# A four-level perceiver kernel: level 0's keys in a new written order, layernorm rows evicted by VectorE, level 3's values dealt out anew

## The chip, the core and the metric

The kernel runs on one core of a Trainium2 chip. The metric is device time in microseconds (us) of one execution; less is better. The core's engines are called by the profile's names: PE (TensorE matmul) with PEld (its weight loads), DVE (VectorE), ACT (ScalarE), POOL (GpSimd) and SP (SyncE, which issues most DMAs). PE writes its results to PSUM, from where DVE or ACT evict them into SBUF.

## What is computed

128 rows x of width 256 (2 batches of 64 latents) pass through twelve residual steps, in four levels of three. Each step adds a function of the layernormed rows:

```
for level in 0..3:
    x = x + xattn(layernorm(x), ctx)   # cross-attention over 2 x 1024 context rows of width 192
    x = x + attn(layernorm(x))         # a mixing of the latents, another kind in each level
    x = x + ffn(layernorm(x))          # a mixture of 8 experts, top 2
```

Three of them matter here. **Level 0's cross-attention** layernorms the context rows too, projects keys from them, divides every 64-wide head of a key by its root mean square, and appends the latents' own keys and values to the context's:

```
k = rmsnorm(heads(layernorm(ctx) @ Wk)) * kn_g
attn = softmax(where(mask, q @ k.T, -max));  out = attn @ v
```

**Level 1's mixing** is a weighted sum over the next 32 rows of the same batch, `out[l] = sum_d softmax(x @ W + b)[l, d] * x[l + d]`. **Level 3's cross-attention** needs `ctx @ Wv`, which depends on no latent and can be computed at any earlier time.

## The kernel before

Everything is fp32. One 128-row tile holds all latents, so each step is a chain of small operations on PE, DVE and ACT, and work that hangs on no latent is put into the gaps of that chain.

**Order.** A Tile scheduler places the instructions on the engines. Inside `in_written_order()` the instructions of PE, DVE, ACT and POOL are tied, engine by engine, to the order in which the program writes them; all of level 0's cross-attention stands inside it, and so does level 1's mixing, while level 1's expert step does not. Each engine works through its queue in order, so an instruction that waits holds up all behind it. DMA issues on SP are not tied.

**Fillers.** A generator such as `kv1.values(b, t)` or `kv3.keys(b, c)` makes a piece of another level's keys or values; `steps(work, n)` advances it by n steps. `values` (line 411) has three: 8 matmuls (`context_values`, lines 373 and 375), 8 more, then one eviction of 128x1024 by ACT (line 437). It takes a PSUM tile of two banks from `two_banks()`, of which there are two (three inside the attention of levels 1 and 3), and gives it back when its eviction is done.

**Level 0's keys** are made in four groups g of four 128-row pieces, and a fifth group, LAT, for the latents. The steps are small functions:

- `project(g)`: 16 matmuls into two banks (lines 373, 375);
- `statistics(g)`: four `bn_stats` and `bn_aggr` on DVE (lines 879, 880), a square root on ACT (line 219), a reciprocal on DVE (line 222), giving `rstd`;
- `take(g)`: four scaled evictions of the projection on DVE (line 901), which need `rstd`; they write one of two `kq` tiles;
- `squares(g)` on ACT (line 911), `sums(g)`: a reduction on DVE (line 916) and a square root on ACT (line 919);
- `over_rms(g)`: three DVE operations (lines 923, 924, 926); `turn_keys(g)`: 8 transposes on PE (line 935) and two evictions on ACT (line 949);
- `normalise_rows(g)` on POOL (line 959), needed only by the later weighing.

`scores(k)`, `softmax(k)`, `turn_p(k)`, `weigh(k)` follow for four units a to d; units a and b need groups 0 and 1 only. ACT's function table is switched by `table_for` (line 214), which runs a one-element activation, `junk`, right behind a table load.

**Turned rows.** `transposed(layernorm(x), 2)` transposes the layernormed rows by two PE transposes (line 247) and evicts them with `evacuate`, which takes DVE (line 102) and ACT (line 104) in turn by a toggle. `layernorm(x, then=F)` puts a square root and then the table load for F on ACT.

**Level 1's attention**, `narrow_attention`, runs 8 rounds over 16 units; each round has on ACT two exponentials (line 1308) and three evictions of transposed weights (line 1332), and PSUM is split so that only two single banks serve transposes (line 1323) and weighing (line 1349). Of level 3's values, the pieces (0,0), (0,2) and (1,0), two halves each, are the fillers from there to level 1's expert step: a half in round 6, one after the last weighing, one ahead of the mixing's layernorm, two after its router matmul, one after its band matmul (line 1495).

**Level 3's experts** run five rounds r; `ways_back()` makes, once, the transposed weights that `scatter(r)` uses, and ends in a matmul (line 755) that waits for an ACT copy (line 754).

Of the kernel before, what the change touches and what calls it, by code (L numbers as in the profile page):

```python
# [11 lines left out]
AF = mybir.ActivationFunctionType  # L12
# [5 lines left out]
P = 128  # L18
# [39 lines left out]
def tile_perceiver(ctx: ExitStack, tc: tile.TileContext, i: dict, out: bass.AP):  # L58
# [39 lines left out]
    def evacuate(dst, src):  # L98

        turn[0] ^= 1  # L100
        if turn[0]:
            nc.vector.tensor_copy(dst, src)  # L102
        else:
            nc.scalar.copy(dst, src)  # L104
# [135 lines left out]
    def transposed(src, n, pool=tok, tag="xT", name="xT"):  # L240

        t = pool.tile([P, n, P], F32, tag=tag, name=name)
        for at in range(0, n, 4):
            m = min(4, n - at)
            ps = bank()
            for c in range(m):
                nc.tensor.transpose(  # L247
                    ps[:, c * P : (c + 1) * P], src[:, (at + c) * P : (at + c + 1) * P], ident
                )
            evacuate(t[:, at : at + m, :].rearrange("p c t -> p (c t)"), ps[:, : m * P])  # L250
        return t
# [127 lines left out]
    class NarrowKeys:  # L379
# [33 lines left out]
        def values(self, b, t):  # L413

            ps = two_banks()
            for u in range(2):
                context_values(ps, self.wv, b, t, (u,))
                yield
            self.evict_values(
                self.v[:, b, :, t : t + 2, :], ps.rearrange("p (n t d) -> p n t d", n=2, t=2)  # L420
            )
            yield
# [131 lines left out]
    def experts(name, x, consts, shelf, blocks, pool, acc, less_sums, bias, b2, sums):  # L554
# [202 lines left out]
        for r in range(OVER + 1):  # L757
            if r:
                sums = sums_of(consts, own_over if r == OVER else consts.of_pair[r])
            prod = hidden(r, sums)  # L760
            if r == 0:
                shelf.load(2)
                shelf.load(3)
            turn(r, prod, 0)
            if r:
                out_of(r - 1)
            if r < OVER:
                gather(r + 1)
            turn(r, prod, 1)
            if r == 0:  # L770
                plan_blocks()
            if r == 1:
                ways_back()
            if r:
                scatter(r - 1)
# [11 lines left out]
    with psum(2, 4), stage_pool(name="l0x", bufs=1) as pool, stage_pool(  # L787
# [288 lines left out]
        statistics(0)  # L1076
        key_bias()
# [7 lines left out]
        statistics(1)  # L1085
        over_rms(LAT)
        sums(0)
        turn_keys(LAT)
        normalise_rows(0)
        normalise_rows(1)  # L1090
        mask_rows()
        a, b, c, d = ((b, j) for b in range(NB) for j in range(2))
        for g in range(4):

            if g > 0 and g < 3:
                statistics(g + 1)
                sums(g)
# [3 lines left out]
            else:  # L1101
                sums(3)
                table_for(AF.Exp, rn[3][:, 0:1])
                scores(a)
                normalise_rows(2)
                normalise_rows(3)
# [3 lines left out]
            if g < 3:  # L1110
                steps(kv1.values(g // 2, 2 * (g % 2)))
            turn_keys(g)
        softmax(a)
# [119 lines left out]
    with psum(2, 4), stage_pool(name="l0f", bufs=2) as pool:  # L1233
        with in_written_order():
            xl = layernorm(x, then=AF.Gelu)
            steps(fill[3], 1)
            xlT = transposed(xl, 2)
# [19 lines left out]
    def narrow_attention(pool, att, x, wq, bq, bv, kv, gap, tail=()):  # L1257
# [120 lines left out]
        with in_written_order():  # L1378
            steps(gap, 3)
            xlT = transposed(layernorm(x, then=AF.Exp), 2)  # L1380
# [8 lines left out]
            for r in range(rounds):  # L1389
# [28 lines left out]
                if r == rounds - 2:  # L1418
                    steps(tail, 1)
# [16 lines left out]
    fill = [kv3.values(0, 0), kv3.values(0, 2), kv3.values(1, 0)]  # L1436
# [14 lines left out]
    with psum(2, 4), stage_pool(name="l1a", bufs=1) as pool, in_written_order():  # L1451
        steps(fill[1], 1)
        xl = layernorm(x, then=AF.Exp)
        xlT = transposed(xl, 2)
# [17 lines left out]
        steps(fill[1])  # L1472
# [51 lines left out]
    with psum(2, 4), stage_pool(name="l2x", bufs=1) as pool, stage_pool(  # L1524
# [5 lines left out]
        with in_written_order():  # L1530
# [3 lines left out]
            xlT = transposed(layernorm(x, then=AF.Exp), 2)  # L1534
# [110 lines left out]
    with psum(2, 4), stage_pool(name="l2t", bufs=1) as pool, stage_pool(  # L1645
# [63 lines left out]
        with in_written_order():  # L1709
            fill = [kv3.keys(0, 0), kv3.keys(0, 1)]  # L1710
            steps(fill[0], 3)
            xlT = transposed(layernorm(x), 2)
# [302 lines left out]
    with psum(2, 4), stage_pool(name="l2f", bufs=2) as pool:  # L2015
        with in_written_order():
            last = kv3.keys(1, 0)
            steps(last, 3)
            xlT = transposed(layernorm(x, then=AF.Silu), 2)
# [53 lines left out]
    with psum(2, 3), stage_pool(name="l3a", bufs=1) as pool:  # L2073
        with in_written_order():
# [4 lines left out]
            xlT = transposed(layernorm(x, then=AF.Sigmoid), 2)  # L2079
# [212 lines left out]
```

## Time and profile before

| | |
|---|---|
| three timed runs | 735.01, 738.56, 739.65 us, median 738.56 |
| the profiled execution, its own time | 738.08 us |
| its span, first to last instruction | 736.4 us |
| mean granted TensorE clock | 0.966 |
| PE, DVE, ACT, POOL busy | 92%, 39%, 36%, 9% of the span |
| level 0's cross-attention | 0 to 90 us of the span, its key preparation to about 53 |
| level 1's attention, mixing, start of its experts | 149 to 201, 201 to 214, 214 to 228 us |
| level 3's experts | 648 us to the end |

A row of a timeline gives the start and the busy time in us, engine, line, operation, output <- inputs, shapes and count; the bracket at its end is the idle time of that engine before it and what ended it. A row of the windows view gives a stretch of the span, then the busy us of PE, PEld, DVE, ACT and POOL with their instruction counts, the granted clock of TensorE (1.00 or 0.50), and the DMA share and rate. The row PEclk of the page shows the same clock in tenths over 40 slices of 18.4 us.

### The profile page before, as it was taken

Reading aid. Unit: us, or ns where it says so; the run is one execution under the profiler, and the core shown is the slowest. Engines: PE = TensorE matmul, PEld = TensorE weight load, DVE = VectorE, ACT = ScalarE, POOL = GpSimd, SP = SyncE. Lnnn points to the kernel's source line nnn. Section 1 sums busy time; section 2 is a strip of 40 time slices with the busy share of each in tenths; the row PEclk is TensorE's granted clock in tenths of the full one; section 3 lists DMA queues with packets and bytes.
Section 4 is the critical chain, followed back from the end, with each engine's and each line's share of the span. In section 5 each row is a group of like instructions: output and inputs, shape, how many; then the busy total and the mean of one; then the engine's idle time right before and its main releaser. Section 6 shows DMA issues by size and latency. Waiting matters only on the chain.

```text
span 736.4 us, 11294 instructions
## 1 busy us (share of the span) xinstructions
PE 676.3 (92%) x4628; PEld 497.2 (68%) x4628; DVE 284.6 (39%) x719; ACT 268.4 (36%) x544; POOL 66.6 (9%) x92
## 2 busy tenths in 40 slices
PE   7779979989969999999999988999999989779997
PEld 3446657946639997576676587999989856544443
DVE  5853443157541003334333335534322267533111
ACT  2353252258543243233232424405231278431111
POOL 3530100000100000000000030030000000000250
PEclk9999999989988999999999999999999999959999
DMA  9930012840004887100000400011138800447881
GB/s 282 423 152 1 8 44 86 291 166 1 3 1 168 293 281 291 53 1 1 1 1 0 172 1 1 1 58 58 58 117 305 308 16 2 161 197 299 341 326 69
DMA packets 19302, 92.76 MB, mean 126 GB/s; under 512 B 3042, under 2 KB 5620, under 8 KB 10324
## 3 DMA queue, kind: packets, MB, share of 16 engines
q1 hardware_dynamic: 16976, 85.70, 31.5%
q0 software_dynamic: 2016, 6.30, 2.3%
q8 instruction: 36, 0.59, 0.3%
q14 instruction: 14, 0.11, 0.0%
q10 hardware_dynamic: 260, 0.06, 0.0%
HBM read 98.20 MB, written 0.13 MB: 134 GB/s over the span
## 4 chain that ended last, share of the span: by engine, by line
PE 83%; DVE 7%; ACT 6%; issue 2%; DMA 0%; POOL 0%; DVEq 0%; ACTq 0%; POOLq 0%
PE bank L255 34%; PE two_banks L574 5%; PE two_banks L1580 4%; PE bank L1323 4%; PE bank L247 3%; PE two_banks L1294 3%; PE bank L619 2%; PE two_banks L1585 2%; PE bank L1349 2%; PE two_banks L1752 2%; PE two_banks L373 2%; PE bank L1872 2%; PE two_banks L399 1%; PE two_banks L255 1%; ACT pT L1332 1%
## 5 line engine op out<-in xcount | busy, mean ns | idle before, releaser
L255 PEld LDWEIGHTS bank<-l2x_ctx,pT 128*128 128x128 f32 x256 | 42.2, 190 | 7.9 <-ACT pT L104 4.9
L255 PE MATMUL bank<-l2x_ctx,pT 128*128 128x192 f32 x256 | 44.4, 327 | 0.6 <-ACT pT L104 0.6
L348 DVE SCALAR_TENSOR_TENSOR x_new<-bank,comb,x_new 128x256 f32<-128x256 f32 x24 | 11.6, 484 | 80.0 <-PE bank L255 80.0
L1323 PEld LDWEIGHTS bank<-ident,p 128*128 128x128 f32 x256 | 29.6, 149 | 18.4 <-issue 6.8
L1323 PE MATMUL bank<-ident,p 128*128 128x128 f32 x256 | 39.5, 298 | 1.2 <-ACT pT L1332 0.5
L1302 DVE TENSOR_REDUCE negmax<-two_banks 128x1 f32<-128x1024 f32 x32 | 37.6, 1216 | 7.3 <-PE two_banks L1294 7.3
L1308 ACT ACTIVATE p<-two_banks,negmax 128x1024 f32<-128x1024 f32 x32 | 36.1, 1127 | 0.8 <-DVE negmax L1302 0.8
L1580 PE MATMUL two_banks<-ctxA,l2x_qA 128*128 128x512 f32 x64 | 32.6, 597 | 0.5 <-DVE l2x_qA L102 0.5
L255 PEld LDWEIGHTS bank<-xT,l1f_w_sb 128*128 128x128 f32 x256 | 32.5, 207 | 0.6 <-issue 0.3
L255 PE MATMUL bank<-xT,l1f_w_sb 128*128 128x128 f32 x256 | 32.8, 291 | 0.0
L1332 ACT COPY pT<-bank 128x512 f32<-128x512 f32 x48 | 26.9, 588 | 15.7 <-PE bank L1323 15.7
L1511 ACT ACTIVATE l1f_hT<-bank,cols 128x128 f32<-128x128 f32 x64 | 18.3, 368 | 35.6 <-PE bank L255 35.6
L255 PEld LDWEIGHTS bank<-xT,l2f_w_sb 128*128 128x128 f32 x256 | 29.6, 192 | 0.3
L255 PE MATMUL bank<-xT,l2f_w_sb 128*128 128x128 f32 x256 | 29.8, 275 | 0.0
L104 ACT COPY pT<-bank 128x512 f32<-128x512 f32 (+1 forms) x22 | 12.1, 557 | 47.8 <-PE bank L247 47.8
L255 PE MATMUL bank<-l1f_w_sb,l1f_hT 128*128 128x256 f32 x128 | 28.8, 379 | 0.0
L1590 DVE TENSOR_REDUCE negmax<-two_banks 128x1 f32<-128x1024 f32 x16 | 19.6, 1225 | 20.8 <-PE two_banks L1585 20.8
L1294 PE MATMUL two_banks<-n_kT,n_qx 32*128 32x512 f32 x128 | 25.0, 680 | 2.8 <-ACT n_kT L434 1.8
L247 PEld LDWEIGHTS bank<-ident,p 128*128 128x128 f32 x164 | 17.7, 141 | 13.8 <-issue 11.8
L255 PEld LDWEIGHTS bank<-l1f_w_sb,l1f_hT 128*128 128x128 f32 x128 | 23.8, 190 | 2.9
L574 PE MATMUL two_banks<-l3f_w_sb,m_xg 128*64 128x512 f32 (+1 forms) x112 | 25.0, 668 | 0.5 <-ACT m_xg L597 0.5
L262 POOL TENSOR_TENSOR x_bias<-x_new,rows 128x256 f32<-128x256 f32 x4 | 2.9, 726 | 242.1 <-DVE x_new L348 237.6
(559 smaller groups left out, 1316.5 us busy)
## 6 DMA issues: line engine op xcount, KB each, us to landing
l1f_w_sb<-in_l1f_w_dram SPq DMA_DIRECT2D x16, 1024.0 KB, 4.8
l3f_w_sb<-in_l3f_w_dram SPq DMA_DIRECT2D x12, 1024.0 KB, 5.7
more_w<-in_l3f_w_dram SPq DMA_DIRECT2D x12, 1024.0 KB, 11.2
l0f_w_sb<-in_l0f_w_dram SPq DMA_DIRECT2D x8, 1024.0 KB, 9.0
l2f_w_sb<-in_l2f_w_dram SPq DMA_DIRECT2D x8, 1024.0 KB, 4.7
l2f_w_sb<-in_l2f_w_dram SPq DMA_DIRECT2D x8, 512.0 KB, 4.6
xh<-in_ctx_dram SPq DMA_DIRECT2D x8, 192.0 KB, 6.0
l2x_ctx<-in_ctx_dram SPq DMA_DIRECT2D x1, 1536.0 KB
```

The costliest lines, as they stand in the source:

```text
L247: nc.tensor.transpose(ps[:, c * P : (c + 1) * P], src[:, (at + c) * P : (at + c + 1) * P], ident)
L255: nc.tensor.matmul(dst, lhsT, rhs, start=(k == 0), stop=(k == len(pairs) - 1))
L373: nc.tensor.matmul(dst[n], ctxA[:, b, n, keys], w[:, 0, :], start=True, stop=False)
L574: nc.tensor.matmul(part[s], xg[r][:, c, s], shelf.at[r, j, n](c, f), start=False, stop=(c == 1), skip_group_check=True,)
L1294: nc.tensor.matmul(sc[u][:, n * 512 : (n + 1) * 512], qx[rows_, c, n, b].rearrange("p h q -> p (h q)"), kT[c, b][rows_, n, :], start=True, ...
L1302: nc.vector.tensor_reduce(sc[u][1], sc[u][0], AX.X, ALU.max, negate=True)
L1308: nc.scalar.activation(p[u], sc[u][0], AF.Exp, bias=sc[u][1], scale=1.0, accum_out=total[u // 4][:, u % 4 : u % 4 + 1],)
L1323: nc.tensor.transpose(ps[:, kc * P : (kc + 1) * P], p[u][:, (4 * k + kc) * P : (4 * k + kc + 1) * P], ident,)
L1332: nc.scalar.copy(dst, ps)
L1511: nc.scalar.activation(hT[:, at + f, :], ps[:, f * P : (f + 1) * P], AF.Gelu, bias=col("l1f_b1", e * 8 + at + f), scale=1.0,)
L1580: nc.tensor.matmul(dst[n], qA[:, j, b].rearrange("p h q -> p (h q)"), ctxA[:, b, n, :], start=True, stop=False,)
L1590: nc.vector.tensor_reduce(negmax, sc, AX.X, ALU.max, negate=True)
```

## The change

Four edits. (1) `evacuate` gets `on_vector`; a new helper `turned_rows` evicts the two transposed layernorm blocks by DVE at nine places (levels 0 and 1's experts, level 1's mixing, both narrow attentions, level 2's three steps, level 3's mixing). The toggle still turns, so no other eviction changes its engine. (2) Level 0's key preparation is written in another order: statistics of group 1 go ahead of the first `take`, later statistics behind the sums of the group before; each value filler is split in two around `turn_keys`, its second half and its eviction now behind; scores and softmax of unit a go ahead of group 3's `over_rms`. (3) Level 3's first piece of values becomes two half pieces with an eviction each, by the new `values_of`; none is left in round 6 of level 1's attention, and three halves stand where the mixing's DVE chain runs, for two before. Level 1's expert step gets a written order for its layernorm. (4) `ways_back` of level 3's experts moves ahead of `out_of(0)` in round 1.

```diff
-    def evacuate(dst, src):
+    def evacuate(dst, src, on_vector=False):
         turn[0] ^= 1
-        if turn[0]:
+        if turn[0] or on_vector:
             nc.vector.tensor_copy(dst, src)
...
+    def turned_rows(xl):
+        return transposed(xl, 2, on_vector=True)
...
+        def values_of(self, b, t):
+            ps = two_banks()
+            context_values(ps, self.wv, b, t, (0,))
+            yield
+            self.evict_values(
+                self.v[:, b, :, t, :], ps.rearrange("p (n t d) -> p n t d", n=2, t=2)[:, :, 0]
+            )
+            yield
...
             turn(r, prod, 0)
+            if r == 1:
+                ways_back()
             if r:
                 out_of(r - 1)
...
-            if r == 1:
-                ways_back()
             if r:
                 scatter(r - 1)
...
         statistics(0)
+        statistics(1)
         key_bias()
...
         squares(0)
         sums(LAT)
-        statistics(1)
         over_rms(LAT)
         sums(0)
-        turn_keys(LAT)
         normalise_rows(0)
         normalise_rows(1)
         mask_rows()
+        turn_keys(LAT)
         a, b, c, d = ((b, j) for b in range(NB) for j in range(2))
         for g in range(4):
-            if g > 0 and g < 3:
-                statistics(g + 1)
-                sums(g)
             if g < 3:
                 take(g + 1, psk)
                 squares(g + 1)
             else:
-                sums(3)
-                table_for(AF.Exp, rn[3][:, 0:1])
-                scores(a)
-                normalise_rows(2)
-                normalise_rows(3)
+                softmax(a)
             if g < 2:
                 psk = project(g + 2)
             over_rms(g)
             if g < 3:
-                steps(kv1.values(g // 2, 2 * (g % 2)))
+                fill = kv1.values(g // 2, 2 * (g % 2))
+                steps(fill, 1)
+                sums(g + 1)
+            if g < 2:
+                statistics(g + 2)
+                normalise_rows(g + 2)
+            if g == 2:
+                table_for(AF.Exp, rn[3][:, 0:1])
             turn_keys(g)
-        softmax(a)
+            if g == 2:
+                scores(a)
+            if g < 3:
+                steps(fill)
         scores(b)
...
-            xlT = transposed(layernorm(x, then=AF.Exp), 2)
+            xlT = turned_rows(layernorm(x, then=AF.Exp))
...
-                if r == rounds - 2:
-                    steps(tail, 1)
...
-    fill = [kv3.values(0, 0), kv3.values(0, 2), kv3.values(1, 0)]
+    fill = [kv3.values_of(0, 0), kv3.values_of(0, 1), kv3.values(0, 2), kv3.values(1, 0)]
...
         steps(fill[1], 1)
         xl = layernorm(x, then=AF.Exp)
-        xlT = transposed(xl, 2)
+        xlT = turned_rows(xl)
         ps = bank()
         accumulate(ps[:, :32], [(xlT[:, c, :], router("l1a", c)) for c in range(2)])
-        steps(fill[1], 1)
-        steps(fill[2], 1)
+        steps(fill[1])
+        steps(fill[2], 2)
...
         nc.scalar.activation(w, w, AF.Exp, bias=nm, scale=1.0, accum_out=tot)
-        steps(fill[1])
+        steps(fill[2])
+        steps(fill[3], 1)
...
         nc.tensor.matmul(ps[:, :D], bandT[:, 0, :], xl, start=True, stop=True)
-        steps(fill[2], 1)
+        steps(fill[3], 1)
         x = residual(x, ps[:, :D])
-        steps(fill[2])
...
-        xlT = transposed(layernorm(x, then=AF.Gelu), 2)
+        with in_written_order():
+            xl = layernorm(x, then=AF.Gelu)
+            steps(fill[3])
+            xlT = turned_rows(xl)
         mix = Mix(x, gate(xlT, "l1f"))
```

More of the change, by code (lines that the diff above doesn't have):

```diff
@@ L238, in layernorm, with transposed @@
         return t
-    def transposed(src, n, pool=tok, tag="xT", name="xT"):
+    def turned_rows(xl):
+        return transposed(xl, 2, on_vector=True)
+    def transposed(src, n, pool=tok, tag="xT", name="xT", on_vector=False):
         t = pool.tile([P, n, P], F32, tag=tag, name=name)
@@ L249, in transposed @@
                 )
-            evacuate(t[:, at : at + m, :].rearrange("p c t -> p (c t)"), ps[:, : m * P])
+            evacuate(
+                t[:, at : at + m, :].rearrange("p c t -> p (c t)"), ps[:, : m * P], on_vector
+            )
         return t
@@ L420, in values @@
                 self.v[:, b, :, t : t + 2, :], ps.rearrange("p (n t d) -> p n t d", n=2, t=2)
+            )
+            yield
[5 more added lines that the diff above has]
+                self.v[:, b, :, t, :], ps.rearrange("p (n t d) -> p n t d", n=2, t=2)[:, :, 0]
             )
@@ L1453, in tile_perceiver @@
         xl = layernorm(x, then=AF.Exp)
-        xlT = transposed(xl, 2)
+        xlT = turned_rows(xl)
         ps = bank()
         accumulate(ps[:, :32], [(xlT[:, c, :], router("l1a", c)) for c in range(2)])
-        steps(fill[1], 1)
-        steps(fill[2], 1)
+        steps(fill[1])
+        steps(fill[2], 2)
         PAD = 32
@@ L1495, in tile_perceiver @@
         nc.tensor.matmul(ps[:, :D], bandT[:, 0, :], xl, start=True, stop=True)
-        steps(fill[2], 1)
+        steps(fill[3], 1)
         x = residual(x, ps[:, :D])
-        steps(fill[2])
     with psum(2, 4), stage_pool(name="l1f", bufs=2) as pool:
-        xlT = transposed(layernorm(x, then=AF.Gelu), 2)
+        with in_written_order():
+            xl = layernorm(x, then=AF.Gelu)
+            steps(fill[3])
+            xlT = turned_rows(xl)
         mix = Mix(x, gate(xlT, "l1f"))
@@ L1533, in tile_perceiver @@
             steps(last, 2)
-            xlT = transposed(layernorm(x, then=AF.Exp), 2)
+            xlT = turned_rows(layernorm(x, then=AF.Exp))
             steps(last)
@@ L1711, in tile_perceiver @@
             steps(fill[0], 3)
-            xlT = transposed(layernorm(x), 2)
+            xlT = turned_rows(layernorm(x))
             psk = project(1)
@@ L2018, in tile_perceiver @@
             steps(last, 3)
-            xlT = transposed(layernorm(x, then=AF.Silu), 2)
+            xlT = turned_rows(layernorm(x, then=AF.Silu))
             steps(last)
@@ L2078, in tile_perceiver @@
             nc.scalar.mul(less_sums, ps[:, :8], -1.0)
-            xlT = transposed(layernorm(x, then=AF.Sigmoid), 2)
+            xlT = turned_rows(layernorm(x, then=AF.Sigmoid))
             psz = features(xlT, wz, 0, 2)
```

## The prediction

> **What bounds the kernel.** The page first: who is busy, and what the chain that ended last is made of.
>
> ```profile
> PE 676.3 (92%) x4628; PEld 497.2 (68%) x4628; DVE 284.6 (39%) x719; ACT 268.4 (36%) x544; POOL 66.6 (9%) x92
> ...
> PEclk9999999989988999999999999999999999959999
> ...
> PE 83%; DVE 7%; ACT 6%; issue 2%; DMA 0%; POOL 0%; DVEq 0%; ACTq 0%; POOLq 0%
> ```
>
> PE carries 83% of the chain, DVE and ACT 13%, DMA nothing. The change removes no matmul, so it can gain in two ways: PE waits less for DVE and ACT, or PE runs less at half clock (the 8s and the 5 of PEclk). Both are read by stage. First the timeline of level 0's preparation, where I look at the brackets.
>
> ```profile
> 31.36 1.27 ACT L949 ACTIVATE kT<-bank,cols 128x512 f32<-128x512 f32 x2
> 32.52 0.30 ACT L219 ACTIVATE root<-cx_mv,eps 128x4 f32<-128x4 f32 x1
> ...
> 32.92 0.18 DVE L222 RECIPROCAL rstd<-root 128x4 f32<-128x4 f32 x1 [2.19 <-ACT root L219]
> ...
> 49.96 0.17 DVE L923 TENSOR_SCALAR rn<-rn 128x16 f32<-128x16 f32 x1 [2.54 <-ACT junk L214]
> ...
> 51.83 1.82 PE L935 MATMUL bank<-ident,kq 128*128 128x128 f32 x8 [1.17 <-DVE kq L926]
> ```
>
> A group's square root stands on ACT behind the key evictions of the group before, so DVE waits 2.19 us for it (2.50 in the next group), and in the last group 2.54 us behind the table load. Then the timeline of level 1, from the attention's end to the experts:
>
> ```profile
> 191.32 1.03 PE L373 MATMUL two_banks<-l3x_wv_sb,ctxA 128*128 128x256 f32 x4
> ...
> 194.24 1.08 PE L1349 MATMUL bank<-pT,n_v 128*32 128x128 f32 x32 [0.24 <-ACT pT L1332]
> ...
> 212.25 0.32 PE L247 MATMUL bank<-ident,l1a_band 128*128 128x128 f32 x1 [2.61 <-DVE l1a_band L1489]
> ...
> 217.58 1.28 ACT L214 ACT_TABLE_LOAD   x1
> ...
> 219.39 1.02 PE L255 MATMUL bank<-routers,xT 128*128 128x8 f32 x4 [2.52 <-ACT xT L104]
> ```
>
> The turned rows of level 1's experts wait on ACT behind a value copy and a table load. Last the windows view, cut into 3.41 us stretches on the grid of the clock's changes:
>
> ```profile
> 48.54:51.95 3.41, 2.24 (x11) 1.20 (x10) 1.92 (x4) 1.38 (x2) 0.00 (x0) 1.00 0.00 0
> 51.95:55.37 3.42, 3.42 (x11) 2.38 (x11) 1.22 (x3) 2.37 (x5) 0.00 (x0) 0.50 0.00 0
> ...
> 215.79:219.21 3.42, 1.09 (x7) 0.50 (x6) 0.46 (x2) 2.63 (x4) 0.00 (x0) 1.00 0.00 0
> 219.21:222.62 3.41, 3.23 (x15) 3.23 (x16) 1.57 (x11) 0.34 (x2) 0.00 (x0) 0.50 0.00 0
> 222.62:226.03 3.41, 3.41 (x18) 3.41 (x18) 0.00 (x0) 1.14 (x4) 0.00 (x0) 0.50 0.00 0
> ...
> 683.42:686.83 3.41, 2.75 (x14) 1.10 (x16) 0.13 (x1) 0.60 (x2) 0.00 (x0) 1.00 0.98 408
> 686.83:690.25 3.42, 3.42 (x10) 0.97 (x8) 0.00 (x0) 0.53 (x1) 0.00 (x0) 0.50 1.02 431
> ```
>
> After a stretch in which PE idles, or runs matmuls of 1 or 8 rows (lines 549's and 993's kind), the next comes at half clock, and it falls on dense work.
>
> **Part by part.** I sum against the profiled execution: 738.08 us, span 736.4.
>
> *Level 0's order.* I step the queues by the rows' durations: statistics 1.84 us, take 1.58 to the next (1.66 to its end), sums 1.2, over_rms 1.75, half a value piece 1.65, a projection 3.3, turn_keys 1.1, two key evictions 1.27, a value eviction 1.0. Stepped so, the old order gives 52.5 for the last turn_keys (trace: 51.83), so I trust differences. Statistics of group 1 (13.4 to 15.3) fit the 2.73 us in which DVE waited for the key bias until 16.16: nothing, if the rows are there; their last DMA issue ends at 7.89 and lands at most 6.0 later, 13.9. Then DVE is through LAT's over_rms 1.8 us earlier (20.3 for 22.1), and the first take starts near 23.6 for 25.24. From there DVE hardly waits: the root has only a short one ahead of it. But PE pays: the first value piece is evicted behind the key evictions, these behind the root (30.6 on ACT), so projection 3, which needs a two-bank tile, starts at 32.5 for 31.52, with PE idle from 30.0. The backlog (3.3 + 3.3 + 1.1 + 1.65 + 1.1, and 1.0 for the next value eviction) puts unit a's scores at 43.9 for 47.28, its softmax on DVE at 47.4, group 3's over_rms behind it at 49.4, the last turn_keys at 50.7 less the model's 0.65: **50.1 for 51.83, -1.7 us**. Which tile the planner hands out isn't in the trace: if projection 3 takes the other one and the third piece need not wait, -2.9; if all the slack goes to PE's waits, 0. I take -1.7. The POOL operations moved (normalise_rows) have until 60 us; SP gets no other order.
>
> *Level 1's attention.* Half a piece leaves round 6: 1.6 us of PE (191.32 to 192.91). What is late next is ACT: exponential 15 ends at 192.47, the eviction that frees the bank for line 1349 would run 192.5 to 193.05 instead of from 193.60. **-1.1.** The rounds behind keep their shape.
>
> *The mixing.* The half piece's own eviction is 0.6 us (128x512, as line 1332's rows) for 1.01, so the square root's table is there in time: -0.15 (root 203.61 while its input was ready at 203.43). Three halves, for two, now stand behind the router's matmul and the exponential, 5.0 us of PE from 204.9 to 209.8 in the shifted timeline; the band is ready at 210.8, so DVE's twelve band steps hide them with 1.0 us to spare, and each microsecond over that would count in full.
>
> *The turned rows.* From PE's transposes to the next matmul: 0.96 us through DVE (150.12 to 151.08), 0.90 through an idle ACT (413.99 to 414.89). Four of nine places were on DVE already. Level 2's and 3's two ACT places lose 0.06 each; level 0's gains 0.07; the mixing's 1.13 becomes 0.96, -0.17; level 1's experts' 2.95 (216.44 to 219.39) becomes 0.96, **-2.0**, and 0.1 more as the transposes no longer wait for the half piece on PE. The value copy that is written there now lies behind the table load on ACT, and its first gelu comes microseconds later. A rule speaks against this: the Trainium skill, *VectorE: DVE Perf Modes*, Specifications, places ScalarE closer to PSUM and VectorE closer to SBUF. By the rule the edit costs, at five places 0.06, +0.3 in all; the row of 2.95 outweighs it, because ACT's copy stands in a queue. The price of that queue differs too: *ScalarE: Activation LUTs*, What ACT_TABLE_LOAD costs, gives about 2.66 us for a switch, 1.38 of it a drain; here the load takes 1.28 and the next activation starts at 218.88, 0.02 later, so the gain is 2.0 and not the 3.4 that the page would make of it.
>
> *ways_back.* Its wait for the ACT copy (0.71 us ahead of 684.08) moves to about 678.8, behind two 0.59 us ACT copies: 0.7 again. Order alone: 0, bounds -0.7 (copy hidden) and +0.6 (one more ACT copy waited for).
>
> Sum of order and eviction: -1.7 - 1.1 - 0.15 - 0.17 - 2.1 + 0.05 = **-5.2**.
>
> *The clock.* Four of its half-clock spells fall where the change works. In level 0, turn_keys takes 1.82 for 1.09 and the scores' main part 2.85 for 1.88: 1.7. At the band matmul, 1.22 for 0.6: 0.6. At the experts' start, 6.6 us of dense PE at half clock: 3.3. In level 3, 32 matmuls of line 574 take 8.78 for 7.09: 1.7. Together **7.3**. The new order fills the stretches before them: unit a's scores and a half piece run where PE idled (43.8 to 46.3); the mixing's 3.3 us hole (208.93 to 212.25) is cut to 1.0, the 2.95 us one to under 1; ways_back no longer adds its 1.06 us of small work to the 8-row matmuls. Here a rule and the rows differ: the Trainium skill, *TensorE: Matmul & The Clock Gate*, What's actually happening, has the half clock after an idle window of about 3.4 us. By the rule only the level 1 spells could go (the stretches ahead of the others hold 2.24 and 2.75 us of busy PE): 3.9. By the rows weak stretches count as well: 7.3. Against that, the new idle 2.4 us ahead of projection 3 could draw a spell, 1.7. The page also says that the windows run free of the kernel, which no run here shows yet; but the grid is arbitrary to the program, so I count two thirds: **-4.8**.
>
> 738.1 - 5.2 - 4.8 = 728.1; the profiled execution lies 0.5 under the median, so **728.5**.
>
> **The rivals.**
>
> *The clock gives nothing* (0.20): spells are lost here and come elsewhere. For it: nine spells in the trace, five of them in places that the change leaves. Against: the two in level 1 follow PE holes of 3.3 and 2.95 us, and both are closed. 738.6 - 5.2 = 733.4, a no-change by measurement.
>
> *Level 0 gives nothing* (0.06): PE's waits for tiles eat the 1.7, and a spell takes the place of the old one. 728.5 + 1.7 + 1.1 = 731.3.
>
> *Slower by a clinging half clock* (0.04): a spell can hold itself, since slow work leaves weak stretches; 645.87 to 662.94 is five in a row. If PE's idle time ahead of projection 3 starts such a spell in level 0, its 16.6 us of PE work to the last turn_keys doubles, less PE's idle time of 2.4, 1.2 and 1.6 us: +11.4 there, and the level 0 gains (1.7 and 1.7, the second by two thirds) are gone: 728.5 + 11.4 + 2.8 = 742.7. It decides from some five windows on; in the trace PE's hole there of 2.3 us (19.9 to 22.26) started none.
>
> That the change doesn't do what it says, by other tiles or by order left to the planner, lies in level 0's bounds.
>
> **How the numbers follow.** Forecast 0.70 (726 to 731), the rivals 0.20, 0.06, 0.04. Low: everything comes, with the other tiles: 738.1 - 5.2 - 1.2 - 7.3 = 724.4, less 0.9 for another run's grid: 723.5. High: order without clock, 733.4, and 1.6 for the three runs' own spread: 735. About 1% (7.4 us) is what a measurement of this kernel can tell from no change. Faster by more: under 731.2, the forecast and a third of the second rival, 0.72. Within: 0.24. Slower: 0.04.
>
> **What would show it.** In the changed profile: the last turn_keys of level 0 near 50; DVE without 2 us waits for roots; PE idle some 2 us ahead of projection 3, with its releaser a value eviction on ACT or a take; in round 7 line 1349 at 1.1 us sooner; turned rows by line 102's copy nine times, router matmul within 1.0 us of the transposes; no 0.50 in the stretches behind the mixing; round 2's 32 matmuls near 7.1 us. I am wrong if level 1's experts start less than 3 us nearer to the attention's end, if new spells at half clock appear in level 0, or if the band's transpose waits for value matmuls.

## The result and the profile after

The changed kernel took **728.3 us** (median of four executions, 727.30 to 731.73) for 738.5 before (735.01 to 739.65): a ratio of 0.9869, 95% interval 0.9831 to 0.9907. Its profiled execution took 727.3 us, with a span of 725.6, 10.8 under that of before, and a mean granted clock of 0.976 for 0.966. First the page of the changed kernel: busy time, the clock in 40 slices, and the chain that ended last.

```profile
PE 670.8 (92%) x4628; PEld 493.7 (68%) x4628; DVE 286.9 (40%) x724; ACT 266.6 (37%) x540; POOL 65.9 (9%) x92
...
PEclk9899999989999999999999999999999999969999
...
PE 85%; DVE 8%; ACT 5%; issue 2%; DMA 0%; POOL 0%; DVEq 0%; ACTq 0%; POOLq 0%
```

The same 4628 matmuls are busy for 5.5 us less, and the span has 34.6 us at half clock for 49.5 before, so about half of the 10.8 us is clock. The 8 in the second slice is new. To see where the time came from, I matched the matmuls of the two traces and followed the distance between their starts:

| from here on | before, us | after, us | shift | new |
|---|---|---|---|---|
| level 0, weights of unit a turned | 58.67 | 57.92 | -0.75 | -0.75 |
| level 0, experts | 121.27 | 118.97 | -2.30 | -1.55 |
| level 1, projection of the attention | 201.16 | 197.46 | -3.70 | -1.40 |
| level 1, band's transpose | 212.25 | 208.84 | -3.41 | +0.29 |
| level 1, experts' router | 219.39 | 213.44 | -5.95 | -2.54 |
| level 1, experts, some 6 us on | 228.38 | 219.26 | -9.12 | -3.17 |
| level 3, round 2 of the experts | 685.86 | 676.11 | -9.75 | -0.63 |
| the same, its matmuls done | 694.16 | 682.71 | -11.45 | -1.70 |
| near the end | 726.46 | 715.68 | -10.78 | +0.67 |

Level 0 gave little, and one gain (-1.55 behind level 0's mixing) lies where nothing was changed. Here is level 0's timeline after the change; lines 965, 453, 379, 917 and 951 are 949, 437, 373, 901 and 935 before.

```profile
30.30 0.30 ACT L219 ACTIVATE root<-cx_mv,eps 128x4 f32<-128x4 f32 x1 [1.65 <-DVE cx_mv L896]
30.51 1.25 ACT L965 ACTIVATE kT<-bank,cols 128x512 f32<-128x512 f32 x2
30.64 0.18 DVE L222 RECIPROCAL rstd<-root 128x4 f32<-128x4 f32 x1 [0.36 <-ACT root L219]
...
31.64 1.01 ACT L453 COPY n_v<-two_banks 128x1024 f32<-128x1024 f32 x1
...
32.71 2.08 PE L379 MATMUL two_banks<-wkc,ctxA 128*128 128x256 f32 x4 [2.72 <-ACT n_v L453]
...
41.86 1.66 DVE L917 SCALAR_TENSOR_TENSOR kq<-two_banks,rstd,bwk 128x256 f32<-128x256 f32 x4 [3.95 <-PE bank L951]
...
52.73 1.09 PE L951 MATMUL bank<-ident,kq 128*128 128x128 f32 x8 [1.47 <-DVE kq L942]
```

DVE's wait for the root fell from 2.19 to 0.36 us. PE pays with 2.72 us ahead of projection 3, and its four matmuls then take 2.08 us where the same form takes 1.13 at full clock. So DVE waits 3.95 us for PE instead, and the last turn_keys comes at 52.73. The timeline of level 1, from round 7 to the experts' router (lines 1369, 251 and 261 are 1349, 247 and 255 before):

```profile
190.53 1.08 PE L1369 MATMUL bank<-pT,n_v 128*32 128x128 f32 x32
...
204.69 1.89 PE L379 MATMUL two_banks<-l3x_wv_sb,ctxA 128*128 128x256 f32 x4
...
208.84 0.33 PE L251 MATMUL bank<-ident,l1a_band 128*128 128x128 f32 x1
...
213.44 0.61 PE L261 MATMUL bank<-routers,xT 128*128 128x8 f32 x4 [0.52 <-DVE xT L102]
```

The router waits 0.52 us for DVE's copy, for 2.52 before. The band's transpose has no bracket: PE came straight from value matmuls, one group of which ran at half clock (1.89 us). The windows view, cut on this execution's grid of clock changes (PE, PEld, DVE, ACT, POOL, clock, DMA):

```profile
28.77:32.19 3.42, 1.22 (x7) 0.48 (x5) 2.84 (x12) 1.88 (x4) 1.21 (x2) 1.00 1.01 422
32.19:35.60 3.42, 2.89 (x8) 1.69 (x8) 3.35 (x6) 1.73 (x3) 3.42 (x3) 0.50 1.00 422
35.60:39.01 3.41, 3.41 (x10) 1.68 (x8) 1.68 (x9) 0.31 (x2) 1.43 (x3) 0.50 1.01 425
...
213.10:216.51 3.41, 3.07 (x27) 3.08 (x28) 1.86 (x12) 1.71 (x5) 0.00 (x0) 1.00 0.00 0
216.51:219.92 3.41, 3.04 (x23) 2.42 (x23) 0.70 (x2) 1.80 (x7) 0.00 (x0) 1.00 0.24 65
...
676.20:679.60 3.40, 3.40 (x22) 1.06 (x16) 0.00 (x0) 0.60 (x1) 0.00 (x0) 1.00 0.92 345
```

Two half-clock stretches follow the new hole in level 0; none is left at the start of level 1's experts or in round 2 of level 3's.

### The profile page after: what moved, and what is told of

Read it like the earlier page. It is cut to its first block, busy times and chain, and to the rows that moved or that the text cites. A ratio compares the mean times of both kernels' runs of the same rounds, so it can differ in the third digit from the quotient of the medians.

```text
span 725.6 us, 11293 instructions
## 1 busy us (share of the span) xinstructions
PE 670.8 (92%) x4628; PEld 493.7 (68%) x4628; DVE 286.9 (40%) x724; ACT 266.6 (37%) x540; POOL 65.9 (9%) x92
## 4 chain that ended last, share of the span: by engine, by line
PE 85%; DVE 8%; ACT 5%; issue 2%; DMA 0%; POOL 0%; DVEq 0%; ACTq 0%; POOLq 0%
PE bank L261 34%; PE two_banks L590 5%; PE two_banks L1601 4%; PE bank L1343 4%; PE bank L251 3%; PE two_banks L1314 3%; PE bank L635 2%; PE two_banks L1606 2%; PE two_banks L379 2%; PE bank L1369 2%; PE two_banks L1773 2%; PE bank L1893 2%; PE two_banks L405 1%; PE two_banks L381 1%; PE two_banks L261 1%
## 5 line engine op out<-in xcount | busy, mean ns | idle before, releaser
L261 PEld LDWEIGHTS bank<-xT,l1f_w_sb 128*128 128x128 f32 x256 | 29.7, 192 | 0.6 <-issue 0.3
L261 PE MATMUL bank<-xT,l1f_w_sb 128*128 128x128 f32 x256 | 30.1, 276 | 0.0
L590 PE MATMUL two_banks<-l3f_w_sb,m_xg 128*64 128x512 f32 (+1 forms) x112 | 23.4, 636 | 0.5 <-ACT m_xg L613 0.5
```

Source lines behind the costliest of these rows:

```text
L261: nc.tensor.matmul(dst, lhsT, rhs, start=(k == 0), stop=(k == len(pairs) - 1))
L590: nc.tensor.matmul(part[s], xg[r][:, c, s], shelf.at[r, j, n](c, f), start=False, stop=(c == 1), skip_group_check=True,)
```

## The experiments

Each was timed against the kernel before on the same chip. Kernels of one group shared a chip; beside the four groups (four, four, three kernels and one) the kernel before had medians of 738.38, 739.2, 736.56 and 737.9 us, so kernels of different groups are compared by their ratios too.

### The four edits, one at a time

Each is a part of the diff shown above, alone on the kernel before.

> Edit (1) alone on the kernel before: the turned layernorm rows leave on VectorE at all nine places, nothing else is moved. Theory (half of the change's gain in level 1 is order, half is clock): from the last weighing of level 1's attention to the dense work of its experts 2.2 us less by order (the experts' router matmul comes within 1.0 us of the transposes, 2.95 before; the mixing's 1.13 becomes 0.96), and the 3.3 us of half clock at the experts' start may go with the 2.5 us hole ahead of it; the hole ahead of the band's transpose stays, and with it its weak stretch. 738.5 - 2.2 = 736.3 without the clock, 733.0 with it. Rival (the clock is chance): 736.3. Rival (VectorE is the slower way out of PSUM and costs at the other places): 737 or above.

> Edit (2) alone: level 0's key preparation in the new order. Theory (the order gains about 2.3 us, and the half clock behind the new hole ahead of projection 3 takes it back): projection 3 near 32.7 with the value eviction as its releaser, the last turn_keys between 49.5 (no stretch at half clock between 32 and 39) and 52.7 (two of them). Time 737.8 with them, 734.5 without. Rival (the order in itself is worth nothing): last turn_keys near 51.8 with full clock between 32 and 39, time 738.5.

> Edit (3) alone: level 3's values dealt out anew and the written order in level 1's expert step, with the turned rows by the toggle as before and the old level 0 and ways_back. Theory: round 7's weighing 1.2 us sooner, the experts' rows still on ScalarE behind a table load and a value copy, so their start no more than 1 us sooner; the hole ahead of the band's transpose 1 us or less. By order 738.5 - 1.2 - 0.2 - 0.8 = 736.3; 0.6 less where the band's product runs at full clock. The 2 us wait for the rows and the weak stretch with it stay, so the dense start of the experts is still at half clock. Rival (the values' place is what keeps the clock up): 3.3 us more, 732.4.

> Edit (4) alone: ways_back ahead of out_of(0). Theory: order nothing (0.7 us of waiting for the ScalarE copy moves with it), the clock 1.7 us in round 2 of level 3's experts if the stretch before it is no longer weak, of which up to 0.7 is given back where PE waits 0.45 us in round 3 while the DMA engines are full: 736.8 to 737.5. Rival (the spell went by the grid's chance): 32 matmuls of round 2 at half clock in part again, 738.5.

| kernel | median, us (runs) | ratio to before | interval |
|---|---|---|---|
| before | 738.38 (55) | | |
| (1) rows by DVE | 733.56 (12) | 0.9936 | 0.9910 to 0.9962 |
| (2) level 0's order | 734.74 (20) | 0.9950 | 0.9930 to 0.9969 |
| (3) values anew | 734.69 (12) | 0.9943 | 0.9919 to 0.9966 |
| (4) ways_back early | 736.99 (20) | 0.9976 | 0.9956 to 0.9995 |

All four gain. Edit (1) gives 4.8 us where its order alone was put at 2.2: the clock theory's 733.0 lies in the interval (731.7 to 735.6), the rivals' 736.3 and 737 above it. In its profile the band's transpose is at 213.93 and the router at 218.50, 4.57 us for 7.14, and the experts behind start at full clock.

Edit (2) gives 3.6 us, between the 0.6 and the 3.9 expected with and without half clock behind the hole. Its profile has one such stretch (33.5 to 37.0) and the last turn_keys at 52.01; level 0 ends 1.5 us earlier. That this profile shows less than the median is answered below: where half clock falls differs from execution to execution.

Edit (3) brings round 7's weighing 1.24 us forward, as in the changed kernel. Its experts' router comes 5.63 us behind the band's transpose, 1.5 less than before; most of that is clock and not its written order, as the next experiment shows. The 3.7 us measured are more than the 2.2 to 2.8 expected. The interval reaches from 2.5 to 6.0, so it doesn't shut out the rival's 732.4 either; in the profile one stretch of half clock is left at the experts' start (220.1 to 223.5), where before has two.

Edit (4) gains 1.4 us. The groups view shows round 2's 32 matmuls, their busy time and the mean of one in ns, before and then with the edit alone; it is clock, 1.7 us in this execution:

```profile
L574 PE MATMUL two_banks<-l3f_w_sb,m_xg 128*64 128x512 f32 x32 | 8.8, 712 | 0.0
```
```profile
L574 PE MATMUL two_banks<-l3f_w_sb,m_xg 128*64 128x512 f32 x32 | 7.1, 595 | 0.0
```

It isn't chance of the grid: of all the profiles of this study, the five with the old place (before, the three other single edits and the next experiment) have a half-clock stretch that begins between 682 and 687 us; the nine with the new place have none there.

These runs also show that the clock's stretches run free of the kernel. Up to 678 us, edit (4)'s kernel is the kernel before. Up to 230 us its half clock begins at 22.9, 53.6, 77.5, 111.7, 162.9 and 214.1 us; in the profile before at 52.0, 110.0, 157.8, 212.4 and 219.2. The offset of the 3.41 us grid was 2.44 here and 0.77 there. So one profile's half clock is one draw. That explains the -1.55 us behind level 0's mixing: half clock comes there in 9 of the 12 profiles of this study that leave the place as it was, and the changed kernel's draw is one of the three without.

### Is it the clock, or only the order?

Five useless matmuls are put into each of PE's two holes in level 1 of the kernel **before** (`keep_busy(n, w, m)` runs n matmuls of 128x256 into a bank that nobody reads):

```diff
+        keep_busy(5, xl[:, :P], xl)
         bandT = transposed(band, 1, pool, "bandT", "bandT")
...
-        xlT = transposed(layernorm(x, then=AF.Gelu), 2)
+        with in_written_order():
+            xl = layernorm(x, then=AF.Gelu)
+            xlT = transposed(xl, 2)
+            keep_busy(5, xl[:, :P], xl)
```

> The kernel before with five useless 128x256 matmuls (2.13 us at full clock, into a bank that nobody reads) in each of PE's two holes in level 1: ahead of the band's transpose (2.61 us of idle PE) and ahead of the experts' router (2.52 us). No step of the kernel's own work is earlier. Clock theory (a stretch of 3.4 us with too little array work is followed by one at half clock): no half clock from 209 to 228, 738.4 - 3.9 = 734.5. Rival (only the order counts, half clock comes where it will): 738.4. Rival (the idle holes aren't free, useless work delays the band and the router): 739 or above.

Measured: 737.29 us (20 runs) for 739.2, ratio 0.9966 (0.9944 to 0.9988). More work made the kernel faster. Its second part also ties the order of the experts' layernorm, but in the traces PE, DVE, ACT and POOL run the same instructions in the same order as before, the useless ones apart, so order can't explain it. The granted clock of the timed runs rose from 0.967 to 0.973. The size, 1.9 us in the medians and 2.5 by the ratio, is under the 3.9 expected. By chance, its grid (offset 2.56) almost equals that of edit (4)'s profile (2.44), whose level 1 mixing is the old one, without filling. So their stretches compare directly; first edit (4), then the filled holes:

```profile
210.67:214.08 3.41, 1.13 (x7) 0.40 (x5) 2.93 (x13) 1.78 (x2) 0.00 (x0) 1.00 0.00 0
214.08:217.50 3.42, 2.71 (x6) 2.02 (x7) 1.41 (x5) 0.00 (x0) 0.00 (x0) 0.50 0.03 7
217.50:220.91 3.41, 2.44 (x8) 0.80 (x6) 0.67 (x3) 1.82 (x3) 0.00 (x0) 0.50 0.00 0
220.91:224.32 3.41, 2.12 (x10) 2.12 (x11) 0.95 (x9) 1.43 (x4) 0.00 (x0) 0.50 0.00 0
```
```profile
210.80:214.22 3.42, 3.42 (x17) 2.22 (x15) 2.94 (x13) 1.79 (x2) 0.00 (x0) 1.00 0.00 0
214.22:217.63 3.41, 2.57 (x12) 1.50 (x11) 1.67 (x6) 0.45 (x2) 0.00 (x0) 1.00 0.01 2
217.63:221.04 3.41, 2.93 (x17) 2.68 (x18) 0.41 (x1) 2.60 (x4) 0.00 (x0) 1.00 0.00 0
221.04:224.46 3.42, 3.42 (x33) 3.42 (x33) 1.57 (x11) 1.34 (x5) 0.00 (x0) 1.00 0.00 0
```

With 1.13 us of PE in the first stretch, four stretches (13.7 us) follow at half clock; with 3.42, none.

The same pair of kernels shows how much of the wait for the experts' rows is clock. First the copy of these rows before, then the band's transpose and the copy with the holes filled:

```profile
218.99 0.35 ACT L104 COPY xT<-bank 128x256 f32<-128x256 f32 x1
```
```profile
214.55 0.30 PE L252 MATMUL bank<-ident,l1a_band 128*128 128x128 f32 x1 [0.25 <-DVE l1a_band L1494]
...
219.91 0.35 ACT L104 COPY xT<-bank 128x256 f32<-128x256 f32 x1
```

From the transpose to the copy it is 6.74 us before (212.25 to 218.99) and 5.36 here, in the same order: at half clock the band's product and the value matmuls are late, and the value copy on ACT, which waits for them, stands ahead of the rows. Edit (3), with its own order, has 5.20. So some 1.4 us of its 1.5 are clock.

### Level 0's hole

Three kernels take the changed kernel's 2.72 us hole apart. Beside them the changed kernel ran once more.

> The changed kernel with the statistics of groups 2 and 3 written behind turn_keys and the value eviction, so that on ScalarE the key evictions and the value eviction no longer stand behind their square root (30.30 us in the trace). Nothing else moves. Theory: the value eviction ends near 31.0, projection 3 starts there for 32.7, the hole ahead of it is 1.0 us for 2.7, the last turn_keys is 1.6 us sooner than 52.7 where half clock still follows, up to 4 us where it doesn't: 726.7, or 724. Rival (the root, 0.7 us later, makes the next take and everything on VectorE late and the last turn_keys stays): 728.3.

> The changed kernel with five useless 128x256 matmuls (2.13 us) in PE's 2.72 us hole ahead of projection 3. Clock theory: no half clock between 32 and 39 us, projections 3's matmuls 1.13 and 0.70 for 2.08 and 1.23, last turn_keys up to 3 us sooner: 725.5 to 726.8. Rival (spells are chance, and the hole only shifts them): 728.3. If the useless work itself runs at half clock it is 4.3 us long and the kernel up to 1.5 us slower, 730.

> The changed kernel once more, unchanged, for its spread and for the place of its half-clock stretches in another execution. Theory (the stretches of the clock run free of the kernel): the half clock lies at other microseconds than 32.2 to 39.0, 155.1 to 161.9 and 202.8 to 206.2, by another offset of the 3.41 us grid, while the order of the instructions and PE's holes are the same; median 728.3, single executions 726 to 732. Rival (the stretches are tied to the program): the same places to a tenth of a microsecond.

The statistics of groups 2 and 3 moved behind (first kernel; the move is shown below for one group) gave 729.44 us (4 runs, 724.98 to 729.84), near the rival's 728.3 and above both figures of the theory. The reason was another than the rival's. Projection 3 came at 31.20, as expected, and no half clock followed in its profile, but now the square root of group 3 stood behind the second value eviction:

```profile
40.23 0.18 DVE L222 RECIPROCAL rstd<-root 128x4 f32<-128x4 f32 x1 [2.24 <-ACT root L219]
```

The last turn_keys came at 51.59, 1.1 us sooner than in the changed kernel; the time doesn't show it, and this execution had more half clock elsewhere (39.6 us in all for 34.6). The filled hole (five matmuls by `keep_busy` ahead of `project(3)`) took 724.88 us (4 runs, three within 724.80 to 724.94), the unchanged kernel beside it 727.94: 3.1 us less, a little more than the clock theory's 1.5 to 2.8. By the ratios it is 2.4 us, and their intervals overlap (0.9767 to 0.9864, 0.9796 to 0.9899), so the times alone don't settle it. The trace does for level 0: the order of the instructions is the changed kernel's, the ten records of useless matmuls apart, its last turn_keys is at 49.51, and the hole's stretches show a busy PE and full clock:

```profile
28.20:31.60 3.40, 3.40 (x18) 2.48 (x17) 2.79 (x12) 1.75 (x5) 0.91 (x1) 1.00 1.01 422
31.60:35.01 3.41, 3.04 (x15) 1.71 (x13) 3.34 (x6) 1.83 (x2) 3.41 (x4) 1.00 0.99 420
```
```profile
32.43 1.13 PE L384 MATMUL two_banks<-wkc,ctxA 128*128 128x256 f32 x4 [0.37 <-ACT n_v L458]
...
49.51 1.09 PE L956 MATMUL bank<-ident,kq 128*128 128x128 f32 x8 [1.47 <-DVE kq L947]
```

The repeated kernel (725.78 to 728.22) drew a grid offset of 1.49, the first had 1.46, so its half clock fell at 32.2 and 155.1 again, as its rival had it. That run alone doesn't part the two; the other profiles do, with offsets from 0.68 to 3.31 us. But it serves as a control: in it the values behind the router ran at full clock, and the band's transpose was in time by 0.91 us:

```profile
208.24 0.30 PE L251 MATMUL bank<-ident,l1a_band 128*128 128x128 f32 x1 [0.91 <-DVE l1a_band L1508]
```

### A better order, more filled holes, and the overlap

```diff
-            if g < 2:
-                statistics(g + 2)
-                normalise_rows(g + 2)
+            if g == 1:
+                statistics(3)
+                normalise_rows(3)
...
             if g < 3:
                 steps(fill)
+            if g == 0:
+                statistics(2)
+                normalise_rows(2)
```

> The changed kernel with only the statistics of group 2 written behind the first value eviction; those of group 3 stay ahead of turn_keys, since with both behind the square root of group 3 stood behind the second value eviction (VectorE waited 2.24 us for it at 40.23 us). No useless work. Theory (the hole ahead of projection 3 is what costs, by its own length and by the half clock behind it): projection 3 at 31.2, last turn_keys near 49.5 for 52.7 and 51.6, median 724.9 to 726, like the kernel with the filled hole. Rival (only the array's load counts, and the 1.1 us hole that is left is still too much of one): half clock between 32 and 39 us again in the profile, 728.

Measured: **724.23 us** (6 runs, 722.71 to 725.93), ratio 0.9837 (0.9807 to 0.9867), with no useless work. The eight executions of the changed kernel lie between 725.78 and 731.73. The timeline of this kernel:

```profile
30.83 1.13 PE L379 MATMUL two_banks<-wkc,ctxA 128*128 128x256 f32 x4 [1.11 <-ACT n_v L453]
...
38.10 0.18 DVE L222 RECIPROCAL rstd<-root 128x4 f32<-128x4 f32 x1 [0.49 <-ACT root L219]
...
40.09 1.13 PE L379 MATMUL two_banks<-l1x_wv_sb,ctxA 128*128 128x256 f32 x4 [1.60 <-DVE kq L917]
...
49.45 1.09 PE L951 MATMUL bank<-ident,kq 128*128 128x128 f32 x8 [1.47 <-DVE kq L942]
```

The hole is 1.11 us, no half clock follows, the second root is in time, and the last turn_keys comes at 49.45. The traces of the two kernels differ in the place of one ACT instruction, the root, and the grid offset, 1.68, is near the changed kernel's 1.46. It was run beside other kernels than the changed one, so the gain over that, 3.7 us by medians, is 0.8 to 2.4 by the ratios to before; the earlier turn_keys is what is sure. But the hole's own length, which the theory counted too, cost nothing: with the hole filled projection 3 started 1.60 us later, at 32.43, and the last turn_keys came at 49.51 all the same. What projection 3 gains here ends in PE's wait of 1.60 us for a take at 40.09 (0.25 with the hole filled). What the hole cost is the half clock behind it.

The next fills more holes of the changed kernel (`keep_busy` takes pairs here; projection 3's hole is filled as above), and the one after it undoes edit (1) in the changed kernel:

```diff
         pT = transposed(p.rearrange("p h t -> p (h t)"), 8, pool, "l0a_pT", "l0a_pT")
+        keep_busy((kT, wo[:, 0, :]), (kT, kT))
         ps = bank()
...
+        keep_busy((kT, wo[:, 0, :]), (kT, kT))
         oT = transposed(o, 4, pool, "l0a_oT", "l0a_oT")
+        keep_busy((kT, wo[:, 0, :]), (kT, kT))
...
             nc.scalar.mul(less_sums, ps[:, :8], -1.0)
+            keep_busy(*[(wz[:, 0, :P], wz[:, 0, :])] * 5)
```
```diff
     def turned_rows(xl):
-        return transposed(xl, 2, on_vector=True)
+        return transposed(xl, 2)
```

> The changed kernel with useless matmuls in PE's holes at three stages: five of 128x256 ahead of projection 3 as before; one of 128x256 and one of 128x128 (0.64 us) in each of the three 0.8 us holes of level 0's mixing (104 to 110 us); five of 128x256 in the 2.58 us hole ahead of level 3's mixing (632 us). No step of the kernel's own work is earlier. Clock theory: beside the 3.1 us at projection 3, the two stretches at half clock that 6 of 10 profiles show behind level 0's mixing (2.8 us where they come) and one of 3.4 us in level 3's mixing (about 1.2) go: 728.2 - 3.1 - 1.7 - 1.2 = 722.2. Rival (half clock that is kept away in one place comes in another, its sum is given): 724.9, as with projection 3's hole alone. If the useless work delays the chains, 726 or more.

> The changed kernel with edit (1) undone: the turned rows leave by DVE and ACT in turn again, all else as changed. The four edits made one at a time gained 4.8, 3.6, 3.7 and 1.4 us, 13.5 together, where all at once gained about 10. Theory (edits 1 and 3 share the wait at the start of level 1's experts, since the written order of edit 3 alone also brings the copy forward): band's transpose to the experts' router 5.6 us for 4.6, the mixing 0.17 more, and half clock at the experts' start in some executions: 728.2 + 1.2 + 0 to 1.7 = 729.4 to 731.1. Rival (the edits add up, the rest is chance of the clock): 728.2 + 4.8 = 733.

More filled holes: 722.78 us (6 runs), ratio 0.9823 (0.9793 to 0.9853). By the median this is the clock theory's 722.2, by the ratio it is 725.4 of 738.5, near the rival's 724.9, so the time doesn't part the two. The granted clock does: 0.983 to 0.986 in the six runs, for 0.979 to 0.981 in the six of the better order, which ran beside them and has no useless work. Half clock that was kept away didn't all come back elsewhere. Its profile has none from 100 to 114 us and none from 632 to 638.

Edit (1) undone: 730.3 us (6 runs), ratio 0.9919 (0.9890 to 0.9949). Its router comes 5.62 us behind the band's transpose, as expected, 4.60 in the changed kernel. So edit (1) is worth 1.0 us there, where it was put at 2.0: the rest is the half clock behind the band's transpose, which is gone in both profiles. The time is in the range of the overlap, but by the ratio it is 732.5 of a 738.5 us kernel, and the interval reaches 734.7; so whether the rest of the 13.5 us is overlap too, or the spread of the five medians, stays open.

Up to 115 us this kernel is the changed kernel, instruction for instruction, but its grid has another offset, 3.31. The hole ahead of projection 3 is as long as there, but a change of windows falls into its middle:

```profile
31.87 1.13 PE L379 MATMUL two_banks<-wkc,ctxA 128*128 128x256 f32 x4 [2.72 <-ACT n_v L453]
...
48.95 1.09 PE L951 MATMUL bank<-ident,kq 128*128 128x128 f32 x8 [1.47 <-DVE kq L942]
```
```profile
27.21:30.62 3.41, 1.93 (x12) 1.15 (x10) 2.80 (x12) 1.37 (x4) 0.48 (x1) 1.00 1.02 428
30.62:34.03 3.41, 2.16 (x10) 1.43 (x11) 3.34 (x7) 2.25 (x3) 3.41 (x3) 1.00 1.02 428
```

No half clock follows, and the last turn_keys comes at 48.95 for 52.73. From the first turn_keys to the last it is 25.33 us in the changed kernel, 22.40 here, 22.40 with the hole filled and 22.33 with it closed. So the hole cost 2.9 us by the half clock behind it, and nothing where it didn't make one window weak.

> What the runs point to, together: the changed kernel with only group 2's statistics behind the first value eviction (724.2 alone), and useless matmuls in the three 0.8 us holes of level 0's mixing and in the 2.58 us hole ahead of level 3's mixing (together 2.1 us in the difference of 722.8 and 724.9), none ahead of projection 3. Clock theory: 724.2 - 2.1 = 722.1, last turn_keys of level 0 near 49.5, no half clock between 100 and 114 us. Rival (what the written order closed, the useless matmuls had already closed, and the clock's sum is given): 724.

Measured: **721.91 us** (6 runs, 719.90 to 724.54), ratio 0.9785 (0.9744 to 0.9827): the lowest median of the study, as the theory's 722.1 had it. Its interval lies below that of the changed kernel's first comparison, but it holds the rival's 724 (0.981 of 737.9) and overlaps with those of the two kernels it is made of; the granted clock, 0.981 to 0.985 for 0.979 to 0.981 with the better order alone, speaks for the theory. The last turn_keys is at 49.99, and the profile has no half clock ahead of 152 us.

## Why the prediction was right

The sum of order and clock was -10.0 us; the span fell by 10.8 and the median by 10.2. The mechanism, PE waiting less and running less at half clock, is what the runs show. That the sum came so near is in part luck: all three signs of being wrong that the prediction named appeared in the first profile. New half clock came in level 0; the band's transpose came straight behind value matmuls; and the experts' router was only 2.25 us nearer to the attention's projection (15.98 for 18.23), where 3 were asked (2.89 in the repeated run). Step by step:

- **Level 0, order -1.7 and clock -1.7 by two thirds.** The steps up to projection 3 held: first take at 23.99 (23.6 foreseen), projection 3 at 32.71 (32.5), and the third value piece waited 0.25 us for a take, not the 1.0 us for a value eviction that the sum had. The forecast of 50.1 for the last turn_keys didn't come in this profile, since half clock did come behind the hole, the danger that was priced at 1.7: two stretches, and level 0 ended 0.75 us sooner for the 2.8 of the sum. In the five profiles without half clock there (hole filled, closed, or open under another grid) turn_keys came at 48.95 to 49.99, in the old order at full clock at 51.83 and 52.28: the order is worth some 2.6 by the means, more than the 1.7. In the three other profiles with the old order a stretch at half clock begins near 23 us and turn_keys comes at 53.2 to 53.5, a spell that the profile before didn't show. Edit (2) alone measured -3.6.
- **Round 7, -1.1:** -1.24.
- **The mixing, -0.15 and -0.17.** From the attention's projection to the router 4.57 us before, 4.26 after: -0.31. The 1.0 us to spare ahead of the band was 0.91 in the repeated run. In the first profile the sign of failure that was named, a band that waits for value matmuls, appeared: router to band took 7.12 us for 6.52. It was half clock on those matmuls, not their number.
- **Level 1's experts, -2.1.** From the band's transpose to the router 7.14 us before, 4.60 after: -2.54, of which 0.6 was put down to the clock. The sum fits, its parts don't: some 1.4 us are clock, by the experiment with the filled holes, and some 1.2 are order, where 2.1 were foreseen, since ACT's value copy had waited for value matmuls at half clock. The 3.3 and 2.95 us that the prediction calls PE holes in level 1 are distances between starts; PE idled 2.61 and 2.52 us in them, by the brackets. The table load took 1.28 us in the changed kernel as well (211.74), and its next activation started 0.01 us later (213.03), so the drain that the Trainium skill, *ScalarE: Activation LUTs*, What ACT_TABLE_LOAD costs, adds wasn't there to be gained.
- **The other turned rows, +0.05.** From the transposes to the next matmul, two places (414 and 589 us of before) lose 0.06 each, level 0's experts (117.6) gain 0.11: nothing in sum. What the Trainium skill, *VectorE: DVE Perf Modes*, Specifications, says, that ScalarE is closer to PSUM, agrees in sign, with that small size.
- **ways_back, order 0:** 0. The +0.67 behind it is a wait of PE in round 3; the repeated run waits 0.95 us, the two kernels with the better order and the two with more filled holes (three kernels in all) not at all. The DMA engines are full there (a share of 0.99 to 1.02 from 690 to 698 us); what PE waits for, no run isolated, and the loss that edit (4)'s expectation put on it didn't show in its own profile.
- **The clock, -4.8.** In the profile, -3.2 in the experts' first 6 us, -1.7 in round 2, -1.55 behind level 0's mixing, +1.5 in level 0 (two new stretches for one and its part), and the mixing's loss. Over all timed runs the granted clock rose from 0.967 (55 runs) to 0.976 (8 runs); were PE busy in all of the difference, 0.009 of 730 us would be 6.6 us, so 4.8 was a fair size. That the steps of the clock came out in other places than named, and the sum held, is partly luck: level 0's loss was made good by the stretch behind level 0's mixing, which this draw lacked and 9 of 12 profiles had.

The rival *the clock gives nothing* (733.4) fell with edit (1), which gained more than its order, and with the filled holes; it lies above the changed kernel's interval too (731.6). The rival *level 0 gives nothing* described this profile of level 0 rightly, spell and all, but not its edit alone. The clinging half clock in level 0 came in no profile; two stretches were the most.

Here rule and rows had differed. By the Trainium skill, *TensorE: Matmul & The Clock Gate*, What's actually happening, half clock follows an idle window; the rows gave it to weak ones too. Round 2's stretch went in nine profiles of nine though PE was busy for 2.75 of the 3.41 us ahead of it: the rows were right. That the windows run free of the kernel, as the page says, the offsets now show.

## What to carry to other kernels

A hole in PE's work can cost more by half clock on the dense work behind it than by its own length, so cost an order by both, and close or fill the holes that stand ahead of dense work. In level 0 the length cost nothing, as other waits took it up, and the half clock 2.9 us. When an eviction is what frees a tile for PE, look at what stands ahead of it on its engine: where the grid made the hole's window weak, one square root written in front of it cost 3.0 us of level 0, by the half clock, and moving a second one behind gave 1.8 of them back. A single profile's half-clock stretches are one draw of the grid; compare them only at the same offset, or count a place over many profiles.

## What the runs showed of the hardware

In these 14 profiles the half clock follows the load of the array and not PE's idle time. For every matmul record I took its free length times its active rows/128 times its active columns/128, and summed over each 3.41 us stretch that begins between 10 and 712 us, a record across a boundary by its part on each side; dense experts reach some 4,100. Below 1,434, 138 of 151 stretches were followed by half clock; from 1,434 to 1,638, 17 of 50; above, none of 2,678. The two limits are read off these profiles. One limit on this load puts 20 of the 2,879 stretches on the wrong side, one on PE's busy time 113, and one on the free length alone, without rows and columns, 83. Rows alone do as well as rows and columns (15), so what the columns count for stays open. So matmuls of 1, 8 or 32 rows keep PE busy but hardly count, as in the changed kernel's start of level 1's attention, where scores of 32 rows keep PE busy for most of 2.27 us:

```profile
151.65:155.06 3.41, 2.27 (x11) 0.60 (x10) 2.24 (x2) 2.94 (x5) 0.00 (x0) 1.00 0.50 173
155.06:158.47 3.41, 3.14 (x10) 1.63 (x11) 2.26 (x3) 1.35 (x4) 0.00 (x0) 0.50 0.00 0
```

The second of these, slowed to half, is busy for 3.14 us and is itself too weak (its sum is some 1,100), so that another at half clock follows.
